# MLP of a convolution-attention pair on one core: second-level input sums handed out by group, and the closing sums of image 0 placed behind the next unit's first layer

## The chip, the cores and the metric

One core of a Trainium2 chip runs the whole kernel. Times are device microseconds (us) of one execution; the time before is the median of three runs. The profile is one further execution, and all places in time are counted from the start of its span.

## The reference

Two layers run one after the other on two images of 512 channels and 32 by 32 pixels. The first is deformable attention with a computed position bias, followed by an MLP with a residual; the second is plain self-attention over the 1024 pixels with a residual. The change lies in the MLP alone. Cut to it:

```python
x   = x + out                                   # attention's output, projected
xn2 = bn(x, bn2_g, bn2_b)
h1  = gelu(einsum('bchw,oc->bohw', xn2, mlp_w1) + mlp_b1)   # 512 -> 2048
x   = x + einsum('bchw,oc->bohw', h1, mlp_w2) + mlp_b2      # 2048 -> 512
# then q, k, v, softmax, output projection and residual of the second layer
```

Everything is float32.

## The kernel before

The kernel has three parts. The first, some 1900 us, computes the position bias of the first layer, in 256 steps (lines 660 to 783). The second is the projection of the attention's output (`project`, line 986 for its matmuls) and the MLP. The third is the second layer's attention (lines 1191 to 1330).

**The MLP is cut into eight units**: four for image 0 (`i` from 0 to 3), then four for image 1 (`i` from 4 to 7). A unit holds 512 of the 2048 hidden channels of one image and has two layers. In the text "unit 4" is the first unit of image 1.

**Both layers use Strassen's scheme**: seven products of blocks instead of eight, with sums of input blocks before and sums of products after. `layer1` uses it twice. The outer scheme needs seven blocks of the normalised input, `xb` (four are written by `normalise`, three are sums, and one of the four is then overwritten by a sum). The inner scheme needs, within each outer block, three sums in `xe` and one in place in `xb`. `spread` issues the four instructions that make such sums, on VectorE; `spread_x` calls it for all of the image: four outer instructions of 128x1024 and three times four inner ones of 128x512, which each take two outer blocks at once. The three pairs of outer blocks are the three groups of `twice`: group 0 uses block slots 1 and 2, group 1 slots 3 and 4, group 2 slots 5 and 6. A sum in slot 5 or 2 may be needed by a later one.

`twice` interleaves the three groups' 21 inner products by the table `STEPS`, in keys of 7 per group. TensorE is held to that order by `tc.issue_after(newest(PE))`. The products go to PSUM, from where ScalarE (lines 165, 169, 171, 175) and VectorE (`plus`, line 137) take them into `hm`. The first four products of a group are number 1, 2, 6 and 5; the addition of product 2 to `d11` on VectorE stands between product 6 and product 5. One more outer product, `second`, is fitted in at key 21, and the layer ends with `spread` on `hm`.

`layer2` forms seven products of `hm` with the second weights, in the order 2, 1, 3, 5, 6, 7, 4. Products 2, 3 and 4 are added to the residual `xs` (`give`). Products 1, 5, 6 and 7 are kept over the four units of an image in the tile `acc` (`own`): in an image's first unit ScalarE copies them there (line 1104), in the others VectorE adds them. The pool gives `acc` one buffer, so both images use the same memory. In the last unit of an image `layer2` also closes the sums: four additions of the bias `mb2` on ScalarE (line 1119) and eight additions of 128x1024 on VectorE, four within `acc` and four from `acc` into `xs`.

**PSUM** is four tiles of two banks, given out in rotation by `Turns`, one of them from the pool `mq` and three from `zp`. Layer 1 takes seven tiles per unit and layer 2 seven, so in unit 4 products 1 and 7 of layer 2 share the tile of `mq`.

**Order on the engines.** The instructions of an engine run one after the other. Their order is set when the kernel is built, by a planner that follows the program order as priority but lets a later instruction go first when an earlier one isn't ready by its own estimate of time; `tc.issue_after` alone fixes an order, on the one engine of the instruction that it names. The queue of VectorE is thus a mixture of all that is listed here.

**Weights.** For each unit SyncE loads the first weights (`load_first`, tiles `w1x` and `w1t` in turn) and the second (`load_second`, `w2t`). GpSimd issues adding DMAs for the weights' outer sums (`gather`, line 942), and after a layer 1 SyncE copies and GpSimd gathers the inner sums `w1e` of the next unit (`load_inner`, line 959 and 942). `w1e` has one buffer. GpSimd sums `w2t` (line 119). A small side product, `wr` (line 1166), runs once per unit on VectorE after layer 1; its buffer is loaded again for the next unit on SyncE.

Of the kernel before, what the change touches and what calls it, by code (L numbers as in the profile page):

```python
# [27 lines left out]
NU = 4  # L28
# [29 lines left out]
def conv_seq_kernel(ctx: ExitStack, tc: tile.TileContext, x, xt, kst, pst, cst, vec, wsm, outw, w1, w2, wl, wlt, brow, out):  # L58
# [62 lines left out]
    def spread(x, which=range(4)):  # L121
        for i in which:
            if i % 2 == 0:
                o, u = ((4, 0), (1, 3))[i // 2]
                nc.vector.tensor_tensor(x[o], x[u], x[1], ALU.subtract)  # L125
            else:
                o, u, v = ((5, 4, 3), (6, 5, 2))[i // 2]
                nc.vector.scalar_tensor_tensor(x[o], x[u], -1.0, x[v], ALU.mult, ALU.subtract)
# [7 lines left out]
    def plus(out, a, b_, op=ALU.add):  # L136
        nc.vector.tensor_tensor(out, a, b_, op)  # L137
# [3 lines left out]
    def twice(pool, sets, weights, moving, dest, done, fills=()):  # L141
        todo = [(7 * g + t, g, q) for g in range(len(sets)) for t, q in STEPS]
        todo += [(t, None, fill) for t, fill in fills]
        held = {}
        for _, g, q in sorted(todo, key=lambda e: e[0]):
            with tc.issue_after(newest(mybir.EngineType.PE)):
                if g is None:
                    q()
                    continue
                if q == 1:  # L150
                    held[g] = pool.tile([P, 2, 512], F32, tag="ps2", name="sw")
                if q == 2:
                    held[g, 2] = pool.tile([P, 2, 512], F32, tag="ps2", name="sw")
                bank = {2: lambda: held[g, 2][:, 0], 5: lambda: held[g, 2][:, 1], 3: lambda: held[g, 2][:, 1]}.get(
                    q, lambda: held[g][:, 0]
                )().rearrange("p (e n) -> p e n", e=2)
                s, t = PARTS[q]
                for e, p in enumerate(sets[g]):
                    nc.tensor.matmul(  # L159
                        bank[:, e, :], weights(p, s), moving(p, t), start=(q in (1, 2, 5) and e == 0), stop=True,  # L160
                        skip_group_check=True,
                    )
            d11, d12, d21, d22 = (dest(g, m, h) for m in range(2) for h in range(2))
            if q == 1:
                nc.scalar.copy(d11, bank)  # L165
            elif q == 2:
                plus(d11, d11, bank)
            elif q == 6:
                nc.scalar.copy(d12, bank)
            elif q == 7:  # L170
                nc.scalar.activation(d22, bank, AF.Copy, scale=-1.0)
                b5 = held[g, 2][:, 1].rearrange("p (e n) -> p e n", e=2)
                plus(d22, d22, b5, ALU.subtract)
            elif q == 4:
                nc.scalar.activation(d21, bank, AF.Copy, scale=-1.0)
            elif q == 3:
                plus(d12, d12, bank)
                done(g)

    FIRST_W, FIRST_X = (1, 0, 2, 3, 4, 5, 6), (1, 4, 0, 6, 5, 2, 3)  # L180
# [754 lines left out]
    with ExitStack() as top, tc.tile_pool(name="wp", bufs=1) as wp:  # L935
# [106 lines left out]
                        )  # L1042
            return go

        def spread_x(xb):
            xe = mp.tile([P, 6, 3, 256], F32, tag="xe", name="xe")
            for g, which in enumerate(((0, 1, 3), (2,), ())):
                spread([xb[:, j] for j in FIRST_X], which)
                spread(inner_x(xb, xe, slice(2 * g + 1, 2 * g + 3), slice(2 * g, 2 * g + 2)))
            return xe  # L1050

        def layer1(p, we, w, xb, xe, hm):
            def gelu(blk, src, scale=1.0):
                for m in range(2):
                    nc.scalar.activation(
                        hm[:, blk, m, :], src[:, m, :], AF.Gelu,
                        bias=col("mb1", 4 * p + 2 * (blk // 2) + m), scale=scale,
                    )

            c11, c12, c21, c22, r5, r3 = (hm[:, j] for j in range(6))  # L1060

            def weights(q, j):
                a = FIRST_W[PARTS[q][0]]
                return inner_w(w, we, a, a - 1)[j]

            def moving(q, j):
                b_ = FIRST_X[PARTS[q][1]]
                return inner_x(xb, xe, b_, b_ - 1)[j]

            def dest(g, m, h):  # L1070
                return hm[:, 2 * g : 2 * g + 2, m, 256 * h : 256 * h + 256]

            def done(g):
                if g == 0:
                    plus(c12, c12, c11)
                elif g == 1:
                    plus(c22, c22, c12)
                    plus(c21, c21, c22)
                    gelu(2, c21, -1.0)
                else:  # L1080
                    plus(c22, c22, r5)
                    gelu(3, c22, -1.0)
                    plus(c12, c12, r5)
                    plus(c12, c12, r3)
                    gelu(1, c12)

            def second():
                ps = mq.tile([P, 2, 512], F32, tag="ps2", name="sw")
                product(w, xb)(ps, 0, 0)
                plus(c11, c11, ps)  # L1090
                gelu(0, c11)

            twice(mq, ((1, 6), (4, 7), (5, 3)), weights, moving, dest, done, ((21, second),))
            spread([hm[:, j] for j in range(7)])

        def layer2(b, p, w, hm):

            if p == 0:
                accs[b] = mp.tile([P, 4, 2, 512], F32, tag="acc", name="acc")

            def own(j):
                a = accs[b][:, j]
                if p == 0:
                    return lambda ps: nc.scalar.copy(a, ps)
                return lambda ps: plus(a, a, ps)

            def give(o2, h, op):
                x_ = xs[:, 2 * o2 : 2 * o2 + 2, b, h * 512 : (h + 1) * 512]
                return lambda ps: plus(x_, x_, ps, op)

            multiply(mq, (2, 1, 3, 5, 6, 7, 4), product(w, hm), {
                1: own(0), 5: own(1), 6: own(2), 7: own(3),
                2: give(0, 0, ALU.add), 3: give(0, 1, ALU.add), 4: give(1, 0, ALU.subtract),
            })
            if p < NU - 1:
                return
            p1, p5, p6, p7 = (accs[b][:, j] for j in range(4))
            for o in range(NCH):
                nc.scalar.activation(xs[:, o, b, :], xs[:, o, b, :], AF.Identity, bias=col("mb2", o))
            v = [xs[:, o2 : o2 + 2, b, n : n + 512] for o2 in (0, 2) for n in (0, 512)]  # L1120
            plus(p6, p6, p1)
            plus(p7, p7, p6)
            plus(v[0], v[0], p1)
            plus(p6, p6, p5)
            plus(p5, p5, p7)
            plus(v[1], v[1], p6)
            plus(v[2], v[2], p7, ALU.subtract)
            plus(v[3], v[3], p5, ALU.subtract)
# [10 lines left out]
        xb = normalise(0)  # L1139
        spread(op1[1])  # L1140
        project(1, *op1, op1w[:, 3:5].rearrange("p a k n -> p a (k n)"))
        xe = spread_x(xb)
        load_second(0)


# [2 lines left out]
        for i, (b, p) in enumerate(units):  # L1148

            j, k = divmod(i, NCH)  # L1150
            if k == 0:
                br = cp.tile([P, C], F32, tag="kz", name="br")
                nc.sync.dma_start(out=br, in_=brow[j].partition_broadcast(P))
            wr = f_pool.tile([P, C], F32, tag="ss", name="wr")
            nc.sync.dma_start(out=wr, in_=wlt[:, i])
            load_first(i + 1)
            if i == 2:
                gg = f_pool.tile([P, 7, 2, 256], F32, tag="vp", name="gg")
                load_g(gg, 0)
            wa, we, wb = wts.pop((b, p))  # L1160
            hm = cp.tile([P, 7, 2, 512], F32, tag="big", name="hm")
            layer1(p, we, wa, xb, xe, hm)
            load_inner(i + 1)

            with tc.issue_after(newest(mybir.EngineType.DVE)):
                nc.vector.scalar_tensor_tensor(
                    wr, wr, 1.0, br, ALU.mult, ALU.mult, accum_out=ub[:, j, k : k + 1]
                )
            if p == NU - 1 and b == 0:
                xb = normalise(1)  # L1170
            layer2(b, p, wb, hm)
            load_second(i + 1)
            if i == NU + 2:
                xbl = blocks(0)
            if p == NU - 1 and b == 0:
                xe = spread_x(xb)
        nc.gpsimd.tensor_tensor(uc, ub[:, 0, 0:2], ub[:, 0, 2:4], ALU.add)
        nc.gpsimd.tensor_tensor(ub[:, 1, :], ub[:, 1, :], vs[:, VOFF["bp"] : VOFF["bp"] + NCH], ALU.add)

# [297 lines left out]
```

## Time and profile before

| what | value |
|---|---|
| three runs | 2640.98, 2643.91, 2644.41 us; median 2643.91 us |
| the profiled execution: its time, its span | 2640.84 us, 2639.0 us |
| TensorE's granted clock, mean | 0.997 |
| unit 0, first layer (first matmul to the second layer's first) | 1945.21 to 1970.22 us |
| unit 3, first layer | 2085.95 to 2107.77 us |
| unit 3, second layer | 2107.77 to 2131.80 us |
| unit 4, first layer | 2131.80 to 2168.02 us |
| unit 5, first layer | 2192.05 to 2214.34 us |

The profiled execution spends 1.84 us outside its span. The first layer does the same matmuls in every unit, so the units can be compared: a longer one holds a wait or a slower clock.

### The profile page before, as it was taken

The page shows a single profiled execution, that of the slowest core. Times are in us where ns is not written, and L with a number is a line of the kernel's source. Part 1 is how long each engine was busy: PE and PEld are TensorE (multiplying, and loading weights), DVE is VectorE, ACT ScalarE, POOL GpSimd, SP SyncE. Part 2 cuts the span into 40 slices and gives each one's busy share as a digit, 9 for nine tenths or more (in the row PEclk, how much of TensorE's full clock was granted, in tenths as well). Part 3 has the DMA queues.
Part 4 walks back from the last instruction along what each step waited for, and adds up shares of the span by engine and source line. Part 5 has one row for each costly group of instructions (what it writes and reads, how often), then busy time and mean ns, then how long its engine had stood idle before and what let it go on. Part 6 is the DMA issues. An engine that isn't in the chain of part 4 may idle for free.

```text
span 2639.0 us, 47884 instructions
## 1 busy us (share of the span) xinstructions
PE 2611.5 (99%) x19656; PEld 995.8 (38%) x19656; DVE 2277.0 (86%) x1425; ACT 1741.6 (66%) x2311; POOL 801.8 (30%) x899
## 2 busy tenths in 40 slices
PE   9999999999999999999999999999999989999999
PEld 3333322333333233333333333333355645646454
DVE  7999999999999999999999999999775685666354
ACT  5887898878888878887887777777632332314041
POOL 1333333333333333333333333333333233200000
PEclk9999999999999999999999999999999989999999
DMA  5788877888878888888887888788778668300000
GB/s 188 176 176 182 192 171 166 179 181 193 181 167 177 180 174 195 180 175 174 173 183 170 176 179 180 170 176 179 192 192 164 128 135 164 68 17 0 32 1 32
DMA packets 164810, 403.53 MB, mean 153 GB/s; under 512 B 24784, under 2 KB 72032, under 8 KB 161904
## 3 DMA queue, kind: packets, MB, share of 16 engines
q0 software_dynamic: 99104, 256.29, 53.3%
q1 hardware_dynamic: 65056, 143.88, 15.9%
q8 instruction: 155, 2.54, 0.4%
q14 instruction: 63, 0.52, 0.1%
q10 hardware_dynamic: 432, 0.31, 0.0%
HBM read 81.10 MB, written 6.55 MB: 33 GB/s over the span
## 4 chain that ended last, share of the span: by engine, by line
PE 91%; DVE 5%; issue 2%; DMA 1%; ACT 1%; DVEq 0%; POOL 0%; ACTq 0%
PE ps L697 63%; PE sw L1191 9%; PE sw L1039 6%; PE sw L159 5%; PE sw L1289 2%; PE sim L783 1%; PE psg L599 1%; PE sw L986 1%; DVE h L680 1%; DMA w1e<-w1e 1%; DVE ub L716 1%; DVE xs L137 1%; DVE hm L137 0%; DVE acc L137 0%; DVE acc L396 0%
## 5 line engine op out<-in xcount | busy, mean ns | idle before, releaser
L697 PE MATMUL ps<-h,cw 128*32 128x512 f32 x16384 | 1775.9, 592 | 4.8 <-ACT rx L706 3.8
L680 DVE CUSTOM_DVE_ANT_1 h<-ta,tb 128x4096 f32<-128x4096 f32 (+1 forms) x257 | 1131.3, 4402 | 29.5 <-PE ps L697 26.5
L697 PEld LDWEIGHTS ps<-h,cw 128*32 128x32 f32 x16384 | 530.7, 110 | 1214.7 <-issue 1153.5
L706 ACT ACTIVATE rx<-ps,sc 128x1024 f32<-128x1024 f32 x512 | 567.7, 1109 | 147.4 <-PE ps L697 125.4
L708 ACT ACTIVATE ub<-ps,sc 128x1024 f32<-128x1024 f32 x256 | 307.9, 1203 | 92.8 <-PE ps L697 92.7
L716 DVE SCALAR_TENSOR_TENSOR ub<-rx,sc,ub 128x1024 f32<-128x1024 f32 x256 | 327.1, 1278 | 6.6 <-ACT ub L708 6.6
L735 POOL DMA_DIRECT2D ua<-uc x126 | 154.0, 1236 | 292.5 <-DMA ua<-uc 285.8
L735 POOL DMA_DIRECT2D ua<-ua x189 | 220.2, 1350 | 24.1 <-DMA ua<-uo 17.3
L718 POOL DMA_DIRECT2D uo<-ub x127 | 122.8, 967 | 246.5 <-DVE ub L716 230.2
L1039 PE MATMUL sw<-hm,w2t 128*128 128x512 f32 x448 | 193.8, 592 | 0.2 <-DVE hm L125 0.2
L708 ACT ACTIVATE uo<-ps,sc 128x1024 f32<-128x1024 f32 x128 | 154.0, 1203 | 52.0 <-PE ps L697 51.7
L716 DVE SCALAR_TENSOR_TENSOR uo<-rx,sc,uo 128x1024 f32<-128x1024 f32 x128 | 163.7, 1279 | 8.4 <-ACT uo L708 8.4
L735 POOL DMA_DIRECT2D uc<-uo x63 | 53.3, 845 | 308.9 <-DMA uc<-uo 308.0
L137 DVE TENSOR_TENSOR hm<-hm,sw 128x512 f32<-128x512 f32 (+1 forms) x80 | 58.8, 738 | 82.0 <-PE sw L159 54.2
L1039 PEld LDWEIGHTS sw<-hm,w2t 128*128 128x128 f32 x448 | 85.0, 190 | 104.3 <-issue 99.0
L137 DVE TENSOR_TENSOR xs<-xs,sw 128x1024 f32<-128x1024 f32 (+1 forms) x48 | 55.7, 1172 | 71.6 <-PE sw L1191 36.0
L718 POOL DMA_DIRECT2D ua<-ub x64 | 58.2, 909 | 176.6 <-DVE ub L716 166.9
L1191 PE MATMUL sw<-aT,vt 128*128 128x512 f32 x224 | 96.7, 593 | 0.3 <-ACT aT L1271 0.3
L660 ACT ACTIVATE ta<-fb,vs 128x512 f32<-128x512 f32 (+1 forms) x65 | 89.2, 1376 | 8.2 <-DMA fb<-fdr 8.2
L708 ACT ACTIVATE ua<-ps,sc 128x1024 f32<-128x1024 f32 x64 | 77.0, 1203 | 20.5 <-PE ps L697 20.1
L708 ACT ACTIVATE uc<-ps,sc 128x1024 f32<-128x1024 f32 x64 | 77.0, 1203 | 20.2 <-PE ps L697 17.1
L165 ACT COPY hm<-sw 128x512 f32<-128x512 f32 x24 | 14.0, 585 | 112.6 <-PE sw L159 112.6
(271 smaller groups left out, 2521.2 us busy)
## 6 DMA issues: line engine op xcount, KB each, us to landing
uo<-ub POOLq DMA_DIRECT2D x127, 512.0 KB, 5.5
fb<-fdr SPq DMA_DIRECT2D x64, 512.0 KB, 5.1
ua<-ub POOLq DMA_DIRECT2D x64, 512.0 KB, 5.5
uc<-ub POOLq DMA_DIRECT2D x64, 512.0 KB, 5.1
ua<-ua POOLq DMA_DIRECT2D x63, 256.0 KB, 6.2
ua<-uo SPq DMA_DIRECT2D x63, 256.0 KB, 2.3
ua<-uo POOLq DMA_DIRECT2D x63, 256.0 KB, 5.7
uc<-uc POOLq DMA_DIRECT2D x63, 256.0 KB, 6.8
```

Source lines behind the costliest of these rows:

```text
L137: nc.vector.tensor_tensor(out, a, b_, op)
L159: nc.tensor.matmul(bank[:, e, :], weights(p, s), moving(p, t), start=(q in (1, 2, 5) and e == 0), stop=True, skip_group_check=True,)
L660: nc.scalar.activation(ta.rearrange("p j x -> p x j")[:, :, j0:j1], fb[:, 0, :, j0:j1], AF.Identity, bias=col("cb1"), scale=col("w1x"),)
L680: nc.vector._custom_dve(TENSOR_ADD_SAT, out=h1[:, y : y + step].rearrange("p y t x -> p (y t x)"), in0=a.unsqueeze(1).to_broadcast([P, ste ...
L697: nc.tensor.matmul(ps[32 * q : 32 * q + 32, h, :], cw2[:, 32 * z : 32 * z + 32], h1[:, 16 * h : 16 * h + 16, q, :], start=True, stop=True,)
L706: nc.scalar.activation(o, ps, AF.Relu, bias=sc[:, 4 + z : 5 + z])
L708: nc.scalar.activation(o, ps, AF.Relu, bias=sc[:, 4 + z : 5 + z], scale=sc[:, z : z + 1])
L716: nc.vector.scalar_tensor_tensor(r[1], r[0], sc[:, z : z + 1], r[1], ALU.mult, ALU.add)
L718: nc.gpsimd.dma_start(out=sums[s][1], in_=sums[s][3], accum_op=ALU.add)
L735: nc.gpsimd.dma_start(out=out, in_=in_, accum_op=ALU.add)
L1039: nc.tensor.matmul(ps[:, m, :], w[:, a, k, m * P : (m + 1) * P], x[:, b_, k, :], start=(k == 0), stop=(k == 1),)
L1191: nc.tensor.matmul(ps[:, m, :], w[:, a, k, c + m * P : c + (m + 1) * P], x[b_][:, k, :], start=(k == 0), stop=(k == nk - 1),)
```

## The change

Two pieces of VectorE work are moved. `spread_x` becomes `sums`, which issues the sums of group 0 at once (outer ones 0, 1 and 3, and the inner ones of slots 1 and 2) and returns a function `part` for the others. In the first unit of each image, `layer1` calls `part(1)` (one outer sum and the inner ones of slots 3 and 4) at key 4 and `part(2)` (the inner ones of slots 5 and 6) at key 10 of the list of `twice`.

The closing sums of an image leave `layer2` and become `finish(b)`. For image 0 it is called after the first layer of unit 4, its VectorE instructions held behind the newest one of VectorE, the last of `spread` on `hm`; for image 1 it is called after the last unit. Two of the eight additions change places. The instruction of `wr` in unit 4 stays behind the newest VectorE instruction, which now is the last of `finish(0)`. No instruction is added or taken away.

```diff
-        def spread_x(xb):
+        def sums(xb):
             xe = mp.tile([P, 6, 3, 256], F32, tag="xe", name="xe")
-            for g, which in enumerate(((0, 1, 3), (2,), ())):
-                spread([xb[:, j] for j in FIRST_X], which)
+
+            def part(g):
+                spread([xb[:, j] for j in FIRST_X], ((0, 1, 3), (2,), ())[g])
                 spread(inner_x(xb, xe, slice(2 * g + 1, 2 * g + 3), slice(2 * g, 2 * g + 2)))
-            return xe
-
-        def layer1(p, we, w, xb, xe, hm):
+
+            part(0)
+            return xe, part
+
+        def layer1(p, we, w, xb, xe, hm, others=()):
...
-            twice(mq, ((1, 6), (4, 7), (5, 3)), weights, moving, dest, done, ((21, second),))
+            twice(mq, ((1, 6), (4, 7), (5, 3)), weights, moving, dest, done, ((21, second), *others))
...
-            if p < NU - 1:
-                return
+
+        def finish(b):
             p1, p5, p6, p7 = (accs[b][:, j] for j in range(4))
...
             plus(p6, p6, p1)
+            plus(v[0], v[0], p1)
             plus(p7, p7, p6)
-            plus(v[0], v[0], p1)
             plus(p6, p6, p5)
...
-        xe = spread_x(xb)
+        xe, part = sums(xb)
         load_second(0)
...
-            layer1(p, we, wa, xb, xe, hm)
+            layer1(p, we, wa, xb, xe, hm, ((4, lambda: part(1)), (10, lambda: part(2))) if p == 0 else ())
+            if i == NU:
+                with tc.issue_after(newest(mybir.EngineType.DVE)):
+                    finish(0)
             load_inner(i + 1)
...
             if p == NU - 1 and b == 0:
-                xe = spread_x(xb)
+                xe, part = sums(xb)
+        finish(1)
```

## The prediction

> **What bounds the kernel now.** I began with the page: TensorE is busy 99% of the span, so only its gaps and slow stretches can be won.
>
> ```profile
> PE 2611.5 (99%) x19656; PEld 995.8 (38%) x19656; DVE 2277.0 (86%) x1425; ACT 1741.6 (66%) x2311; POOL 801.8 (30%) x899
> ```
>
> The view of waits over the MLP (1940 to 2330 us) names them. Columns: waiting line, releaser, sum, times, longest.
>
> ```profile
> PE sw L159 <- DVE hm L137: 15.4, 2, 12.3
> PE sw L159 <- DMA w1e<-w1e: 0.2, 1, 0.2
> ```
>
> TensorE's timeline places both long waits: the first layers of unit 0 and unit 4, before inner product 5 of group 0. Columns: start, duration, group, idle before it.
>
> ```profile
> 1951.14 1.13 PE L159 MATMUL sw<-xe,w1e 128*128 128x256 f32 x4 [3.04 <-DVE hm L137]
> ...
> 2131.80 1.89 PE L159 MATMUL sw<-xb,w1x 128*128 128x256 f32 x8
> 2133.56 1.13 PE L159 MATMUL sw<-xe,w1e 128*128 128x256 f32 x4
> 2147.03 2.07 PE L159 MATMUL sw<-xe,w1e 128*128 128x256 f32 x4 [12.35 <-DVE hm L137]
> ```
>
> VectorE's timeline shows what stands ahead of the awaited addition (2146.30, product 2 to `d11`):
>
> ```profile
> 2132.33 1.22 DVE L137 TENSOR_TENSOR xs<-xs,sw 128x1024 f32<-128x1024 f32 x1
> 2133.46 1.22 DVE L137 TENSOR_TENSOR acc<-acc 128x1024 f32<-128x1024 f32 x1
> 2134.60 0.68 DVE L125 TENSOR_TENSOR xb<-xb 128x512 f32<-128x512 f32 x1
> 2135.20 1.22 DVE L137 TENSOR_TENSOR acc<-acc 128x1024 f32<-128x1024 f32 x1
> 2136.34 3.49 DVE L137 TENSOR_TENSOR xs<-xs,acc 128x1024 f32<-128x1024 f32 x3
> 2139.74 0.68 DVE L128 SCALAR_TENSOR_TENSOR xe<-xe,xb 128x512 f32<-128x512 f32 x1
> 2140.35 1.22 DVE L125 TENSOR_TENSOR xb<-xb 128x1024 f32<-128x1024 f32 x1
> ...
> 2146.30 0.68 DVE L137 TENSOR_TENSOR hm<-hm,sw 128x512 f32<-128x512 f32 x1
> ```
>
> The starts give the pace: 1.135 us for 1024 elements, 0.60 us for 512. From 2132.33 to 2146.30 are 13.97 us: one last addition of unit 3 (1.13), five closing additions (5.67), two sums of group 0 (1.2), and the sums of groups 1 and 2 (1.14 + 8 x 0.60 = 5.94). Product 2 itself was done at 2131.80 + 1.73 = 2133.53.
>
> The table by windows adds a second cost, in its clock column (the last but two):
>
> ```profile
> 2132.00:2136.00 4.00, 2.69 (x12) 1.82 (x10) 4.00 (x5) 3.00 (x4) 1.47 (x1) 1.00 1.01 286
> 2136.00:2140.00 4.00, 0.00 (x0) 0.00 (x0) 4.00 (x5) 0.24 (x1) 2.64 (x1) 0.66 0.84 119
> 2144.00:2148.00 4.00, 0.97 (x2) 0.83 (x3) 2.98 (x5) 0.00 (x0) 3.92 (x2) 0.50 0.00 0
> ```
>
> TensorE stopped at 2134.69; the clock halved at 2137.3, and the first matmuls after the gap run at half speed. Against unit 3's first layer (21.82 us), unit 4's (36.22) has 14.40 us in excess: 12.35 of wait, the remaining 2.05 mainly clock. Unit 0's (25.01) has 3.19.
>
> **What the Trainium skill says.** "TensorE: Matmul & The Clock Gate", section "Architectural detail", says that VectorE and ScalarE are strict first-in-first-out. The trace agrees: the addition at 2146.30 had its product for 12.8 us. The same page, Part 1, puts the clock gate on a free-running window of about 3.4 us: the gap of 12.35 halved the clock, that of 3.04 did not (1.00 throughout). "GPSIMD Engine Reference", section "Specifications", says that GpSimd shares its SBUF interfaces with VectorE instructions of two SBUF inputs. Agreed: four sums of `w2t` took 13.93 us at 2137.36, beside a full VectorE, and 5.06 us in unit 3.
>
> **The change, part by part.** The instructions are the same ones, so what counts is place.
>
> *Sums by group, unit 0.* Six 512-sums stand between 1946.8 and 1950.41, after product 2 could be added (1947.0). If they follow that addition, the excess of 3.19 falls to about 0.5, keeping one sum that the planner still puts in front: **-2.7**. Bounds: -3.2, or nothing, since the moved sums are ready early and may fill the same places. Cover: VectorE's idle stretches in this first layer (2.71, 2.70, 2.69 us). Group 1 needs its outer sum 4.3 us after the layer's start; before, it was already made at 1934.75.
>
> *Sums and closing additions, unit 4.* With three closing additions also gone from before 2132 (3.4 us), group 0's sums (1.2) are done earlier, and the `d11` addition follows the last of unit 3 at about 2133.6. Unit 3's own first layer is the model: a wait of 0.23, in the 21.82. For one 512-sum in front I leave 0.6, and 0.2 for the two bias instructions on ScalarE (1.09 each, not held back by the change), which can fall between copies. Excess 14.40 becomes 0.8: **-13.6**. Bounds: -14.4, and -9 if the early-ready sums stay ahead (5.94 less what fits elsewhere). The 5.94 us of sums fit into 4.50 + 2.70 + 2.70 us of idle time in unit 4's first layer.
>
> *The closing additions in their new place.* In the times of before, `spread` on `hm` ends at 2178.79; eight additions end at 2187.9. VectorE was idle from 2180.5 to 2192.25, so its time is free. But `acc` has one buffer: ScalarE's first copy for image 1 must wait for the last reader of image 0's.
>
> ```profile
> 2175.09 1.01 ACT L1104 COPY acc<-sw 128x1024 f32<-128x1024 f32 x1 [1.08 <-PE sw L1039]
> ```
>
> This copy moves from 2175.09 to 2187.9 and ends at 2188.9. Behind it on ScalarE are the three other copies. It holds product 1's PSUM tile, which product 7 takes next; product 7, the sixth at 3.433 us each from 2168.02, was due at 2185.2. TensorE waits about **+3.8**. The trace of before shows no such wait. Lower bound 0, if only the quarter `p1` is waited for (read last by the second addition, near 2181); the trace speaks for the whole buffer: SyncE's first copy into `w1e` always starts 0.19 us after the last matmul that reads any of it. Upper bound 4.9, if the ready addition of product 3 (1.13) slips among the eight. The clock can halve in this wait: 0 to 2.05 us by the other gaps; 3.8 us span two of the skill's windows, and about half of the phases leave one nearly empty: **+1.0**.
>
> Also behind `finish(0)` on VectorE: `wr` (to 2188.5), whose buffer SyncE refills. On SyncE the next load, `w2t`, came at 2192.29 and is not delayed; the product is next needed at 2225. The addition of product 3 ends near 2189.7, before product 4 wants its tile at 2192.4. `finish` issues no DMA. It is moved past SyncE's load and GpSimd's four sums of `w2t` for unit 4, which touch other buffers and, with a less crowded VectorE, end by 2151 at the latest; product 3 wants them at about 2160. At the end, `finish(1)` lies beside the next stage's matmuls, as before: 0.
>
> *What is late next.* Unit 5 waits for `w1e` (landed 2201.3; excess 22.29 - 21.82 = 0.47). The chain of DMAs starts at unit 4's layer end and now gets 3.8 us more: **-0.5**. In unit 4 the last gather landed at 2138.7, wanted at 2131.80 + 8.9 = 2140.7: cost 0. In unit 1 it landed at 2001.7, wanted at 2003.1; the chain moves forward 1.8 of the 2.7 us, leaving 0.5: cost 0, at worst 2.
>
> Sum: -2.7 - 13.6 + 3.8 + 1.0 - 0.5 = **-12.0 us**. The profiled 2640.84 becomes 2628.8. The median of the runs lies 3.07 higher, so 2643.91 - 12.0 = 2631.9, say 2632.
>
> **The rivals.**
>
> *The wait for `acc` is hidden* (only a quarter is waited for, or TensorE does product 4 first, or the clock holds): -2.7 - 13.6 - 0.5 = -16.8, to -18.1 with nothing left in either gap, hence 2626 to 2627. For it: the idle VectorE. Against: the shared tile.
>
> *The change does only half of what it says*: the planner puts ready sums where they were. The closing additions still go. Unit 0 gives 0, unit 4 -9, less 4.8 for `acc`: -4.2; with unit 5 and some of the sums moved, -4 to -7, hence 2637 to 2640. For it: before, a sum of group 2 already ran at 1926.45, ahead of group 0's.
>
> *Slower: the wait for `acc` grows past the gain.* Place: the copy at line 1104. It costs the end of `finish` plus 1.0 less 2185.2. The gain without it is 16.8, so it decides once `finish` ends after 2185.2 - 1.0 + 16.8 = 2201.0, 13.1 us later than I have it: eleven or twelve more 1024-additions in front. With fifteen in front the kernel is some 4 us slower, and, with a halved clock, 6: 2650. Against it: at 2180.5 the queue ran empty, and only `wr` and two additions compete.
>
> **How the numbers follow.** My forecast 0.62, the hidden wait 0.17, the half change 0.15, slower 0.06. About 0.2% (5.3 us) is what a measurement of this kernel can tell from no change. The half change lies two thirds beyond it (0.10), one third within (0.05); slower divides 0.05 and 0.01. Faster 0.62 + 0.17 + 0.10 = 0.89, same 0.06, slower 0.05. The range takes in the hidden wait, the bounds of `acc` and the clock, and the better part of the half change: 2626 to 2638.
>
> **What would show it.** Right: in unit 0 and unit 4 the wait before product 5 of group 0 is under 1 us; unit 4's clock stays 1.00 in the first layer; eight additions follow `spread` in unit 4; ScalarE's first line 1104 copy waits for VectorE, and TensorE stands 3 to 5 us before product 7; unit 5 no longer waits for `w1e`. Wrong: sums still ahead of the `d11` addition, a wait for `w1e` or `w2t` in units 1 or 4, or a wait before product 7 beyond 6 us.

## The result, and the profile after

The changed kernel takes 2628.36 us (median of four runs, 2627.55 to 2631.86), the kernel before 2643.22 (2640.98 to 2644.41). The ratio is 0.9947, with a 95% interval of 0.993 to 0.9965: 14.9 us faster, against a forecast of 12.0. The profiled execution took 2631.86 us (span 2630.1) and is the longest of the four; what sets it apart is the first thing to look for. The page's first line hardly moves, as TensorE's gaps are small beside its 2600 us of work:

```profile
PE 2612.4 (99%) x19656; PEld 995.4 (38%) x19656; DVE 2278.3 (87%) x1425; ACT 1742.0 (66%) x2311; POOL 795.9 (30%) x899
```

TensorE's timeline (start, duration, group, idle before it) shows both long waits gone, and three new ones of over 1 us:

```profile
1946.06 2.29 PE L159 MATMUL sw<-xe,w1e 128*128 128x256 f32 x8
...
1993.68 1.97 PE L159 MATMUL sw<-xe,w1e 128*128 128x256 f32 x8 [1.03 <-DMA w1e<-w1e]
...
2003.79 2.07 PE L159 MATMUL sw<-xb,w1e 128*128 128x256 f32 x4 [2.89 <-DMA w1e<-w1e]
2005.66 4.78 PE L159 MATMUL sw<-xb,w1t 128*128 128x256 f32 x12
...
2138.82 1.13 PE L159 MATMUL sw<-xe,w1e 128*128 128x256 f32 x4 [0.17 <-DVE hm L137]
...
2157.89 20.76 PE L1039 MATMUL sw<-hm,w2t 128*128 128x512 f32 x48
2180.03 3.70 PE L1039 MATMUL sw<-hm,w2t 128*128 128x512 f32 x8 [1.38 <-ACT acc L1107]
```

In unit 0, products 6 and 5 of group 0 run as one group of eight matmuls (1946.06). In unit 4, 12.35 us of wait have become 0.17. ScalarE's first copies of image 1 wait for `acc`, and that holds TensorE for 1.38 us before the product that it does last in unit 4's second layer. The two waits for `w1e` are in unit 1, which had none before; the twelve matmuls after the second take 4.78 us, where the twelve in the same place take 2.75 in unit 2. The clock column (last but two) of the table by windows says why; it is at 1.00 in the stretches before and after these:

```profile
2002.00:2006.00 4.00, 2.21 (x5) 1.83 (x6) 0.10 (x1) 0.00 (x0) 3.49 (x3) 0.61 0.10 13
2006.00:2010.00 4.00, 4.00 (x11) 3.13 (x10) 2.50 (x3) 1.18 (x2) 0.00 (x0) 0.53 0.00 0
```

VectorE's timeline in unit 4 shows what took the place of the old queue:

```profile
2137.48 0.68 DVE L125 TENSOR_TENSOR xb<-xb 128x512 f32<-128x512 f32 x1
2138.08 0.68 DVE L137 TENSOR_TENSOR hm<-hm,sw 128x512 f32<-128x512 f32 x1
2138.68 0.68 DVE L128 SCALAR_TENSOR_TENSOR xe<-xe,xb 128x512 f32<-128x512 f32 x1
...
2168.58 1.22 DVE L137 TENSOR_TENSOR acc<-acc 128x1024 f32<-128x1024 f32 x1
...
2171.99 1.21 DVE L137 TENSOR_TENSOR xs<-xs,sw 128x1024 f32<-128x1024 f32 x1
...
2176.53 2.35 DVE L137 TENSOR_TENSOR xs<-xs,acc 128x1024 f32<-128x1024 f32 x2
2178.80 0.68 DVE L1172 SCALAR_TENSOR_TENSOR wr<-wr,br 128x512 f32<-128x512 f32 x1
2179.41 1.21 DVE L137 TENSOR_TENSOR xs<-xs,sw 128x1024 f32<-128x1024 f32 x1
```

One sum stands directly ahead of the awaited addition (2138.08) and five stand behind it; the others had run before product 2 was there. The eight closing additions run from 2168.58 to 2178.80, and among them, at 2171.99, the addition of product 3. ScalarE's copies into `acc` follow at once, the first three back to back:

```profile
2178.97 2.84 ACT L1107 COPY acc<-sw 128x1024 f32<-128x1024 f32 x3 [15.09 <-DVE xs L137]
2183.77 1.01 ACT L1107 COPY acc<-sw 128x1024 f32<-128x1024 f32 x1 [1.96 <-PE sw L1039]
```

The last copy, of product 7, starts only when TensorE ends the layer at 2183.57, and the addition of product 4 runs at 2179.41. So TensorE did product 4 sixth and product 7 last, against the written order.

The lengths of the layers, in us, read off TensorE's timeline in one profiled execution of each kernel (L1 and L2: first and second layer of a unit; an undisturbed L1 is 21.82, an undisturbed L2 24.03; all layers not listed are within 0.5 of these):

| kernel | unit 0 L1 | unit 1 L1 | unit 2 L1 | unit 4 L1 | unit 4 L2 | unit 5 L1 | median, us |
|---|---|---|---|---|---|---|---|
| before | 25.01 | 21.82 | 21.82 | 36.22 | 24.03 | 22.29 | 2643.22 |
| changed | 22.32 | 28.99 | 21.82 | 22.13 | 25.68 | 21.82 | 2628.36 |
| again | 22.00 | 24.00 | 21.82 | 22.38 | 25.67 | 21.82 | 2628.19 |
| finish_only | 27.09 | 21.82 | 21.82 | 23.34 | 25.67 | 21.82 | 2630.81 |
| sums_only | 22.00 | 26.21 | 21.81 | 35.10 | 24.03 | 22.18 | 2639.05 |
| gg_late | 22.00 | 21.82 | 23.56 | 22.13 | 25.67 | 21.82 | 2626.94 |
| gg_sums_late | 21.99 | 21.82 | 21.82 | 22.14 | 25.68 | 21.81 | 2624.95 |
| acc_split | 21.99 | 26.08 | 21.82 | 22.14 | 24.03 | 22.34 | 2626.76 |
| p7_first | 22.00 | 25.56 | 21.82 | 22.14 | 30.57 | 21.82 | 2632.98 |
| gg_last | 22.00 | 21.81 | 21.82 | 22.14 | 25.68 | 21.82 | 2624.45 |
| best | 22.01 | 21.82 | 21.82 | 22.37 | 24.03 | 22.13 | 2623.46 |
| before_gg_last | 26.68 | 21.81 | 21.81 | 36.18 | 24.03 | 22.09 | 2642.11 |

Against before, the changed kernel's row gives -2.7, +7.2, -14.1, +1.65, -0.5: -8.4, and with small differences elsewhere the 8.9 us between the two spans. The row "again", the changed kernel once more, has +2.2 in unit 1: -13.5, against 13.4 between the spans (2625.6). The first profiled execution of the changed kernel was thus longer than this one by unit 1 and little else.

### The profile page after: what moved, and what is told of

Same layout as the page of the kernel before. It is cut to its first block, busy times and chain, and to the rows that moved or that the text cites. A ratio compares the mean times of both kernels' runs of the same rounds, so it can differ in the third digit from the quotient of the medians.

```text
span 2630.1 us, 47885 instructions
## 1 busy us (share of the span) xinstructions
PE 2612.4 (99%) x19656; PEld 995.4 (38%) x19656; DVE 2278.3 (87%) x1425; ACT 1742.0 (66%) x2311; POOL 795.9 (30%) x899
## 4 chain that ended last, share of the span: by engine, by line
PE 92%; DVE 3%; DMA 2%; ACT 1%; issue 1%; POOL 0%; DVEq 0%; POOLq 0%; SPq 0%; ACTq 0%
PE ps L697 65%; PE sw L1198 9%; PE sw L1039 5%; PE sw L159 5%; PE sw L986 2%; PE sw L1296 2%; PE sim L783 1%; PE psg L599 1%; DMA w1e<-w1e 1%; DVE hm L137 1%; DMA w1e<-w1t 0%; DVE h L680 0%; DVE xs L137 0%; DVE acc L137 0%; PE pkv L533 0%
## 5 line engine op out<-in xcount | busy, mean ns | idle before, releaser
L165 ACT COPY hm<-sw 128x512 f32<-128x512 f32 x24 | 14.1, 586 | 110.0 <-PE sw L159 110.0
```

## The experiments

Each was run with the kernel before beside it on the same chip; the medians of before in the three groups of runs are 2642.47 us (again, finish_only, sums_only, gg_late), 2641.87 (gg_sums_late, acc_split, p7_first, gg_last) and 2641.98 (best, before_gg_last). The edits are shown shortened, against the changed kernel where nothing else is said.

**The changed kernel once more.** No edit.

> The changed kernel once more, unaltered, to see which of its stages repeat. Theory: unit 1's late inner weights (w1e) are a fixed consequence of the new order, so its first layer again takes well over the 21.82 us of an undisturbed unit (24 to 29). Rival: that wait was an accident of the one profiled execution, and the first layer takes 21.8 to 22.5 here. Both: unit 4's first layer 22.1, unit 0's 22.3; time 2627 to 2632 us.

2628.19 us (ratio 0.9947, 0.9934 to 0.9959). Unit 1's first layer takes 24.00 us, with one wait of 2.12 for `w1e` and the clock at full speed throughout. The wait is part of the new order: it repeats in all five profiled executions that give out the sums by group and leave `gg` (a tile that only the third part needs; more of it below) where it was. How much it costs differs (the layer takes 24.0 to 29.0), by how late the last transfer lands and by whether the clock halves.

**The closing sums alone.**

```diff
-  layer1(..., ((4, lambda: part(1)), (10, lambda: part(2))) if p == 0 else ())
+  layer1(..., ())
   xe, part = sums(xb)
+  part(1); part(2)          # at both places
```

> The closing sums are moved behind unit 4's first layer, but all input sums are given out at once, as before. Theory: this part carries nearly all of the gain: unit 4's first layer about 23.3 us (36.2 before; some 1.2 of sums still stand ahead of the awaited addition), its second layer with a short wait of 1.5, unit 0 unchanged at 25.0, unit 1 unchanged at 21.8; 11 to 12 us under the kernel before, 2631 to 2632 us. Rival: the sums by group carry half of it, and this part alone gives 6 to 8 us (2635 to 2637).

2630.81 us (0.9956, 0.9944 to 0.9969): 11.7 under before, as the theory had it. Unit 4's first layer is 23.34, with a wait of 1.37; the planner, free to do so, had let the awaited addition pass three of the sums anyway. Unit 1 is untouched. The miss is unit 0: 27.09 us instead of 25.0. The wait is the 3.04 us of before, but this time the clock halved behind it:

```profile
1953.46 1.13 PE L159 MATMUL sw<-xe,w1e 128*128 128x256 f32 x4 [3.04 <-DVE hm L137]
1954.43 4.44 PE L159 MATMUL sw<-xb,w1x 128*128 128x256 f32 x12
```

**The sums by group alone.**

```diff
-  if i == NU:
-      with tc.issue_after(newest(mybir.EngineType.DVE)): finish(0)
   layer2(b, p, wb, hm)
+  if p == NU - 1: finish(b)
...
-  finish(1)
```

> The input sums are given out by group, but the closing sums of image 0 stay at the end of its last unit. Theory: unit 0's first layer 22.3 us (25.0 before), given back in unit 1, whose inner weights come late (first layer 24 to 29); unit 4's first layer shortens by at most the 5.9 us of its moved sums and, the closing sums being still ahead, keeps a wait of 6 to 8 and the halved clock; in all 1 to 5 us under the kernel before, 2638 to 2642 us. Rival: the two parts are alternatives, each enough for unit 4 by itself, and this one gives 10 us or more (2633 or less).

2639.05 us (0.9988, 0.9981 to 0.9995), 3.4 under before. Unit 0 wins 3.0 and unit 1 gives back 4.4 in the profiled execution (2642.01 us, one of the longer among 21 runs of 2636.62 to 2643.84). Unit 4 wins only 1.1: the first wait falls by 6.0, but the sums now late raise two others, and the first four matmuls after the wait take 2.08 us, as after the gap of 12.35, where they take 1.13 in the changed kernel: the clock halves again, and a second time after the last of these waits (0.57 from 2154 to 2158).

```profile
2143.46 2.08 PE L159 MATMUL sw<-xe,w1e 128*128 128x256 f32 x4 [6.39 <-DVE hm L137]
...
2150.80 1.10 PE L159 MATMUL sw<-xe,w1e 128*128 128x256 f32 x4 [0.88 <-DVE xe L128]
2153.71 1.72 PE L159 MATMUL sw<-xe,w1e 128*128 128x256 f32 x4 [1.81 <-DVE hm L137]
```

So the closing sums carry most of the gain. The sums by group win 3.4 us by themselves and 2.6 on top of the closing sums (2630.81 to 2628.19); that the two figures differ is not shown, as they lie within the noise of each other.

**Why are unit 1's inner weights late? The load and sums of `gg` moved into unit 2.**

```diff
   if i == 2:
-      load_g(gg, 0)
+      with tc.issue_after(newest(SP)), tc.issue_after(newest(Pool)):
+          load_g(gg, 0)
```

> The changed kernel, with the load and the four GpSimd sums of gg (wanted in the third part of the kernel only) held behind unit 2's own weight load, where the program has them; the planner had drawn them into unit 0. Theory: those sums stood ahead of the last gather of unit 1's weights on GpSimd, and so made unit 1's inner weights late; unit 1's first layer falls to 21.8 to 22.5 us and the kernel to 2621 to 2625 us. Rival: the lateness comes from the transfers of unit 0 and 1 themselves, or was an accident; then 2627 to 2629 us, as the changed kernel.

2626.94 us (0.9943, 0.993 to 0.9955). Unit 1's wait is gone, but the time misses the expected 2621 to 2625: unit 2 now waits twice for its `w1e` (0.95 and 0.47; 23.56 us). The cost moved along with the block, and here it seems to be that of the loads: SyncE issues them from 2017.38 on, right behind its copies into `w1e`, and GpSimd's next gather for `w1e` waits 5.94 us for such a copy. In the next run the sums stand at nearly the same place (from 2035.3, here from 2037.4), the loads are back in unit 0, that gather waits 3.22 us, and unit 2 loses nothing. The expectation also leaned on the 7.2 us of the first profile, the largest of the five; "again" has 2.2.

**The sums or the transfers?** The loads of `gg` stay in unit 0; only its four sums on GpSimd are held behind unit 2's weight gathers.

```diff
   load_g: (loads only)
   if i == 2:
+      with tc.issue_after(newest(Pool)): fold(nc.gpsimd, gg)
```

> The changed kernel with the loads of gg in unit 0, as the planner draws them, and only its four sums on GpSimd held behind unit 2's weight gathers. Theory: the sums on GpSimd ahead of the last gather are what made unit 1's inner weights late, so unit 1's first layer is 21.8 to 22.2 us though the loads are still there; units 2 and 3 may lose up to 2 us to the sums' new place. Rival: the loads' traffic is the cause, and unit 1 stays at 24 us or more.

2624.95 us (0.9936, 0.9923 to 0.9948), unit 1 at 21.82, and nothing lost in unit 2. So unit 1's wait comes from the sums' place in GpSimd's queue. In the kernel before, GpSimd's and then SyncE's timelines read:

```profile
1960.27 5.39 POOL L119 TENSOR_TENSOR gg<-gg 128x512 f32<-128x512 f32 x4
1965.61 0.83 POOL L942 DMA_DIRECT2D w1t<-w1t  x1
```

```profile
1969.55 0.34 SPq L949 DMA_DIRECT2D w1x<-in_w  x1
1970.41 3.99 SPq L959 DMA_DIRECT2D w1e<-w1t  x3
```

in the changed kernel, GpSimd, then SyncE:

```profile
1959.59 7.36 POOL L119 TENSOR_TENSOR gg<-gg 128x512 f32<-128x512 f32 x4
1966.89 0.86 POOL L942 DMA_DIRECT2D w1t<-w1t  x1
```

```profile
1965.63 0.35 SPq L949 DMA_DIRECT2D w1x<-in_w  x1
1974.43 3.08 SPq L959 DMA_DIRECT2D w1e<-w1t  x3
```

and in this run, GpSimd, then SyncE:

```profile
1963.43 0.85 POOL L946 DMA_DIRECT2D w1t<-w1t  x1 [2.73 <-DMA w1t<-w1t]
```

```profile
1966.85 0.35 SPq L953 DMA_DIRECT2D w1x<-in_w  x1
1967.72 3.94 SPq L963 DMA_DIRECT2D w1e<-w1t  x3
```

Without the sums the last gather of unit 1's outer weights (`w1t`) is issued at 1963.43, well ahead of the 1.8 MB load of `w1x`, and SyncE's copies start 0.2 us after unit 0's first layer, as in the other units. With them, in the changed kernel, it is issued 1.3 us after that load and takes 7.4 us to land, where it takes 3.3 us in the kernel before and in this run; the copies, which wait for it, start 7.8 us after the layer. Whether the later gather or the earlier load would do this harm alone was not tried.

**The buffer of the kept products.** `acc` as four tiles of a quarter, in the same memory.

```diff
-  accs[b] = mp.tile([P, 4, 2, 512], F32, tag="acc", name="acc")
+  accs[b] = [mp.tile([P, 2, 512], F32, tag=f"acc{j}", name=f"acc{j}") for j in range(4)]
```

> The changed kernel with acc as four tiles of a quarter each, one buffer each, in the same memory. Theory: the wait in unit 4's second layer (25.67 us there, 24.03 elsewhere) is for the release of acc as a whole; by quarters, the first copy waits only for the second closing sum, and the layer falls to 24.03 to 24.2 us; the kernel to 2626 to 2627 us. Rival: the second copy, whose quarter is read last, holds the same PSUM rotation, and 25 us or more remain.

Unit 4's second layer is 24.03 us and its wait is gone; 2626.76 us (0.9947, 0.9934 to 0.9959) lies within the expectation, though 0.5 comes back in unit 5 as a wait for `w1e`. ScalarE's first copy no longer waits for the last closing addition. The other three start only at 2174.36, as the seventh of the eight ends, without harm:

```profile
2167.55 1.01 ACT L1107 COPY acc<-sw 128x1024 f32<-128x1024 f32 x1 [7.15 <-DVE xs L137]
2174.36 3.01 ACT L1107 COPY acc<-sw 128x1024 f32<-128x1024 f32 x3 [5.80 <-DVE xs L137]
```

**The order of products.** TensorE held to the written order in unit 4's second layer (each product's matmuls in `tc.issue_after(newest(PE))`).

> The changed kernel with TensorE held to the written order of products (2, 1, 3, 5, 6, 7, 4) in unit 4's second layer. Theory: there the planner had put product 4 ahead of product 7, since product 3's PSUM tile came free before product 1's; in the written order TensorE waits 4.5 to 5.2 us before product 7, with up to 2 us more where the clock halves: second layer 28.8 to 31 us, kernel 2631 to 2634 us. Rival: the order was as written and product 7 found another tile; the layer stays at 25.7 us and the kernel at 2628.

30.57 us in that layer, 2632.98 us in all (0.9968, 0.9956 to 0.9981). Five products of eight matmuls, then:

```profile
2154.11 17.33 PE L1039 MATMUL sw<-hm,w2t 128*128 128x512 f32 x40
2176.25 8.60 PE L1039 MATMUL sw<-hm,w2t 128*128 128x512 f32 x16 [4.81 <-ACT acc L1107]
```

The wait before product 7 is 4.81 us, and products 7 and 4 take 8.43 us up to the next layer's start (2184.68), 1.56 more than two at the usual 3.433: the clock had halved (0.60 from 2176 to 2180). The planner's exchange of products 4 and 7 saves 4.9 us.

**`gg` where no gathers compete.** The block `if i == 2` becomes `if i == len(units) - 1`, held back as in gg_late.

> The changed kernel with the load and the sums of gg held back into the last unit, in which neither SyncE nor GpSimd has other weights to fetch. Theory: with them away from all gathers of inner weights, the first layers of units 1 and 2 both take 21.8 us (24.0 to 29.0 and 21.8 in the changed kernel; 21.8 and 23.6 with the sums in unit 2), so 2625 to 2626.5 us. Rival: gg then comes late for the third part, which waits for it, and the kernel is not faster than 2628.

2624.45 us (0.9935, 0.9921 to 0.9948), half a microsecond below the expected range; units 1 and 2 are both undisturbed, and the third part has no wait for `gg`.

**Both remedies, and a control.** "best" joins gg_last and acc_split; "before_gg_last" makes gg_last's edit in the kernel before.

> The changed kernel with gg in the last unit and acc as four tiles. Theory: the gains add: unit 1's first layer 21.8 us and unit 4's second layer 24.0 us, with 0.5 us given back in unit 5, whose inner weights have less time again; about 1.1 us under gg_last, 2623.0 to 2624.0 us. Rival: freed from one wait, unit 5's weights take it all back, and the time equals that of gg_last.

2623.46 us (0.9929, 0.9915 to 0.9943), the lowest median here: 1.0 under gg_last, with 0.3 given back in unit 5. The two were measured on different chips and their runs overlap (2622.81 to 2624.43, and 2624.1 to 2625.1), so the total alone doesn't show this last microsecond; unit 4's second layer does (24.03 against 25.68).

> The kernel before, with gg held back into the last unit and nothing else. Theory: before the change unit 1's inner weights arrived in time (first layer 21.82 us), so that gg's place cost nothing there and moving it gives nothing: within 1 us of the kernel before, 2641 to 2643 us. Rival: gg's place was a cost in itself, and moving it gives 2 us or more.

2642.11 against 2641.98 us (ratio 1.0, 0.9992 to 1.0008). In the kernel before, the place of `gg` cost nothing that can be measured; it does once unit 0 ends its first layer earlier.

## Why the prediction was right, and where it was not

**Unit 0 (-2.7): right.** -2.7 in the changed kernel's profile, -3.0 in "again". The size of the old wait was judged by one execution: with the clock halved, as in two of three executions that still have it (finish_only, before_gg_last), it costs 1.7 to 2.1 us more. In such executions the change wins that too, so the profile of before, with its clock at 1.00 in this layer, was a cheap one to subtract from; how often the kernel before halves there is not known.

**Unit 4's first layer (-13.6): right**, -14.1 and -13.8. One sum in front of the awaited addition was assumed, and one is there. finish_only and sums_only show that the closing additions were the share that counts, and that taking away the other one alone wins 1.1.

**The wait for `acc` (+3.8 and +1.0 for the clock): the mechanism right, the size wrong.** The term that failed is "product 7, the sixth". The release of the whole buffer is shown by acc_split, the shared PSUM tile by p7_first. With the order that was assumed the wait is 4.8 and the layer 6.5 us longer, near the stated upper bounds (4.9 for the wait, 2.05 for the clock). But the planner let product 3's addition slip among the closing ones, product 3's tile came free, and product 4 ran first. Product 4 first was one of the ways named in the hidden-wait rival. Measured: 1.38 of wait, a clock of 1.00 where the estimate by windows had put +1.0, and +1.65 in all instead of +4.8.

**Unit 1's weights (0, at worst 2): wrong.** They were named as what comes late next, and a wait for them among the signs of being wrong, but the step "the chain moves forward 1.8 of the 2.7 us" failed. The chain moved back 4.0 us, from SyncE's copies at 1970.41 to 1974.43, while TensorE came 3.6 us earlier. The step took over the last gather's transfers from before, where they end at 1968.4 (by the view of transfers they count as landed only at 1968.9, 3.3 us after the issue, so that 1.3 us was there to win and not 1.8). But VectorE was now busy through most of the four sums of `gg` (from 1960.47 to 1966.95 without a pause, where before it had an idle stretch of 2.69 us), and these took 7.36 us instead of 5.39, so the gather left at 1966.89 instead of 1965.61; and the load of `w1x`, which before followed 3.9 us behind the gather, now left 1.3 ahead of it. The prediction had seen GpSimd's sums slowed beside a full VectorE, but reckoned with it for `w2t` alone. Measured +2.2 to +7.2 in five profiled executions.

**Unit 5 (-0.5): right**, 22.29 to 21.82; acc_split, which takes the extra time away again, brings the wait back (22.34). The control, before_gg_last, speaks for the same coupling in unit 1: where unit 0 ends late, the place of `gg` costs nothing.

That the total came near is in part luck: the two errors, 3.2 too much for `acc` and 2 or more too little for unit 1, cancel. The gain of 14.9 us (14.3 in "again") lies about as far from the forecast's 12.0 as from the 16.8 of the hidden-wait rival, so the total doesn't tell the two apart; the layers do, and they show a wait for `acc` that was mostly hidden and one for `w1e` that neither had. The slower rival is refuted at its place: behind `spread` stood the eight closing additions and one more, 10.2 us in all, not the twenty that it needed.

## What to carry to other kernels

When a wait goes on the engine that bounds the kernel, everything that was timed by its end comes earlier except what hangs on a fixed chain; follow each transfer of the next stage back to its first issue, with all that stands ahead of it in the issuing engine's queue, not only to its landing time before. Work that isn't wanted for long is best held back by hand from a queue that feeds the critical chain: here four sums wanted 360 us later cost 2 to 7 us by the profiles, and 3.7 by the medians (2628.19 to 2624.45). And where several products share few PSUM tiles, ask whether the order is fixed: a planner that may exchange two products turned 6.5 us into 1.65.

## What the runs showed of the hardware that was not expected

A gap of 3.04 us on TensorE can leave the clock alone (1.00 in the kernel before, 25.01 us) or halve it (27.09 and 26.68 us in finish_only and before_gg_last), in nearly the same place of the program. In unit 1 a gap of 2.07 us halved it in p7_first (0.86 and 0.71 in the two stretches of 4 us from 1992 on), and one of 2.12, before the same product, did not in "again" (1.00). Of the eight gaps between 2 and 3.1 us in the units of these profiles, six halved the clock.

The halved clock comes in pieces of one length. Read in half-microsecond windows, it stands at half speed from 1954.8 to 1958.2 in finish_only, from 1994.9 to 1998.3 in p7_first from 2003.0 to 2009.8 in the changed kernel, and from 2137.3 to 2150.9 in the kernel before, where the gap was 12.35 us: 3.4 us, or twice or four times as long. This fits the free-running window of about 3.4 us that the Trainium skill describes ("TensorE: Matmul & The Clock Gate", Part 1): where the gap falls would count beside its length, so that a wait of 2 to 3 us has two prices, 1.5 to 2 us apart. The phase of the window itself was not measured. The same page lets the clock halve after at least one idle window; here the measurement differs, as gaps of 2.07 to 3.05 us, shorter than a window, were enough.

VectorE and GpSimd slow each other. Two VectorE additions of 128x1024 ran beside the sums of `gg`: they took 2.33 us (at 1961.27) and 1.69 in the changed kernel, and 1.23 and 1.70 in "again". The same two take 1.23 and 1.22 in gg_last, where no sums run beside them. The sums themselves took 5.4 us in the old order and 7.4 in the new one.
